# Layer 2's attention scores: three-part bfloat16 rows and one bfloat16 product in place of float32 products

## The chip, the cores and the metric

The kernel runs on one core of a Trainium2 chip. A core has a matrix engine (PE, whose weight loads are listed apart as PEld), a vector engine (DVE), a scalar engine (ACT), a general engine (POOL) and a queue that issues transfers (SP). Each engine works through its own instructions in a fixed order and waits on semaphores for what others make. Products land in PSUM[...]; everything else on the chip lies in SBUF. The metric is the device time of one execution, in microseconds (us); less is better.

## The reference

The input is 128 graphs of 128 nodes with 128 features, and an adjacency matrix for each. Four layers follow one another, each of the form x = x + gnn(relu(layernorm(x))). Layer 0 scores all pairs of nodes through a small network with a batch normalisation, layer 1 is an attention with eight heads and a second attention on top of it, layer 2 is a single attention, and layer 3 scores by edge type. Cut to what the change touches, layer 2 is

```python
f1 = h @ a1                       # h: [graph, node, 128], a1 and a2: [128, 1]
f2 = h @ a2
e = leaky_relu(f1 + swapaxes(f2, 1, 2), 0.2)
scores = where(adj > 0, e, -9e15)
attention = softmax(scores, axis=2)
return elu(attention @ h)
```

So the score of a pair of nodes is the sum of one number of each node, and everything after it (mask, exponential, weighted sum) starts from that.

## The kernel before

**Stages.** After a setup that loads and rearranges the weights, layer 0 takes about the first 2080 us. The function `layers` then does the rest of the network in one pass over 32 groups of four graphs (`GC` = 4). Nothing of this pass leaves the chip until a group's result is stored.

**The path of a group** is the generator `group`: layer 0's end, normalisation and transposition of h; values and scores of layer 1 by head (`pf`, `f`, `f1d`, `fl`, then `head_attention` for each graph, forked); ELU; a second attention (`z2`); normalisation; layer 2 (`z3`, `single_head`); normalisation; layer 3; store. In layer 2 the features `hv` are transposed into `h2T` (features on the partitions, four graphs side by side, 512 columns), ACT copies them out of PSUM (L953), and then line L1268 and its neighbours form the scores of the four graphs, key nodes on the partitions and query nodes in the columns, in one PSUM bank:

```python
yield PE, 2.0, "ps", "t"
z = psum("z3")
nc.tensor.matmul(z, a1bc, h2T, start=True, stop=False)
for i in range(GC):
    nc.tensor.matmul(z[:, i, :], h2T[:, i, :], a2c.to_broadcast([P, P]), start=False, stop=False)
masked(z, lambda: mask)
```

`a1bc` (L306) holds a1 in each of its 128 columns, so that the first product writes a query's f1 into every partition; the second, with a2 broadcast, adds a key's f2. `masked` (L958) adds a very large negative number where there is no edge, by a bfloat16 product of a scaled identity with the mask. In `single_head`, ACT then takes two exponentials of `z` (L970), with slopes 1 and 0.2, DVE takes their maximum (L962), and PE forms the weighted sum (L1006). A float32 product appears in the profile as two instructions, a bfloat16 product as one.

**Layer 1 has a form of its own for the same task.** `fw` holds the columns that give f1 and f2 of four heads, three times each, so that L1173 writes 24 rows per graph and half of the heads into a strip of 32 partitions. Four vector instructions (L1183 to L1186) then turn each set of three equal rows into three bfloat16 parts whose sum is the float32 number. The masks of rows `of_f1`, `of_f2` and `parts_m` say which row is which. L1194 writes rows with ones where the other factor stands, and L1068 multiplies, so that one bfloat16 product gives f1 + f2.

**What sets the order.** The instructions of PE, ACT, DVE and POOL are in an order written by a small planner, `in_order`, when the program is built. Each `yield` of a generator announces a step: its engine, an assumed cost in us, the buffers that it takes and those that it frees. The planner always picks the step that can begin first by its assumed costs, with six groups under way (`UNDER_WAY`) and a limited number of buffers of each kind: four PSUM banks of kind "ps", two pairs of banks "pz", 28 tiles "t", eleven "w", and so on. A changed cost or a new step therefore changes the order of all later steps. DMAs go through SP and POOL; each group's four inputs are loaded one group ahead.

Of the kernel before, what the change touches and what calls it, by code (L numbers as in the profile page):

```python
# [9 lines left out]
F32 = mybir.dt.float32  # L10
I32 = mybir.dt.int32
I16 = mybir.dt.int16
BF16 = mybir.dt.bfloat16
AF = mybir.ActivationFunctionType
ALU = mybir.AluOpType
AX = mybir.AxisListType
PSUM = bass.MemoryType.PSUM

P = 128
# [7 lines left out]
GC = 4  # L27
NH, DH = 8, 32
HH = NH // 2
# [3 lines left out]
C_T, C_W, C_V, C_O, C_M = 28, 11, 3, 6, 7  # L33
# [13 lines left out]
PE, ACT, DVE, POOL, DMA = "PE", "ACT", "DVE", "POOL", "DMA"  # L47
# [105 lines left out]
def bcast(ap, pos, n):  # L153

    dims = [list(d) for d in ap.ap]
    return bass.AP(tensor=ap.tensor, offset=ap.offset, ap=dims[:pos] + [[0, n]] + dims[pos:])
# [3 lines left out]
def kernel(ctx: ExitStack, tc: tile.TileContext, x, adj, w, out):  # L160
    nc = tc.nc
# [7 lines left out]
    def cst(name, shape, dtype=F32):  # L169
        return const.tile(shape, dtype, tag=name, name=name)  # L170

    ident = cst("ident", [P, P])
# [43 lines left out]
    w1c = cst("w1c", [P, NH, DH])  # L216
    fw = cst("fw", [P, 2, 32])
    w2g = cst("w2g", [P, 2, P + 2])
    a1bc = cst("a1bc", [P, P])
    a2c = cst("a2c", [P, 1])  # L220
    aq = cst("aq", [P, NT, P])
    aqb = cst("aqb", [P, NT])
    vpw = cst("vpw", [P, P])
    parts_m = cst("parts_m", [P, 2])
    of_f1 = cst("of_f1", [P, HH + 1])
    of_f2 = cst("of_f2", [P, HH + 1])
    one = cst("one", [P, 1])
    nc.vector.memset(one, 1.0)
    minus_one = cst("minus_one", [P, 1])
# [7 lines left out]
    with tc.tile_pool(name="wload", bufs=2) as wl, tc.tile_pool(  # L237
        name="wps", bufs=2, space=PSUM
# [24 lines left out]
        for m in range(2):  # L263
            prod = wl.tile([P, NH, DH], F32, tag="prod", name="prod")
            nc.vector.tensor_tensor(prod, w1c, a1b[:, :, m * DH : (m + 1) * DH], ALU.mult)
            for s in range(2):
                for k in range(3):
                    e = (3 * m + k) * HH
# [9 lines left out]
        for m, dst in ((0, of_f1), (1, of_f2)):  # L278
            rows = of_32[:, 3 * HH * m : 3 * HH * (m + 1)]
# [21 lines left out]
            nc.vector.tensor_reduce(gw, prod2, AX.X, ALU.add)  # L301
            nc.vector.tensor_copy(w2g[:, :, P + s], gw)

        acol = wl.tile([P, 1], F32, tag="acol", name="acol")
        nc.sync.dma_start(acol, w["L2_gnn_a1"])
        nc.vector.tensor_copy(a1bc, acol.to_broadcast([P, P]))  # L306
        nc.sync.dma_start(a2c, w["L2_gnn_a2"])


        araw = wl.tile([P, P, NT], F32, tag="araw", name="araw", bufs=1)  # L310
# [119 lines left out]
    with tc.tile_pool(name="h_pool", bufs=1) as h_pool, tc.tile_pool(name="pairs", bufs=B_V) as b_v:  # L430
# [10 lines left out]
        with tc.tile_pool(name="a2", bufs=2) as a2, tc.tile_pool(  # L441
            name="a_d", bufs=A_D
        ) as a_d, tc.tile_pool(name="a_ph", bufs=3, space=PSUM) as a_ph, tc.tile_pool(
            name="a_ps", bufs=2, space=PSUM
# [144 lines left out]
            with tc.manual_schedule(engines=ORDERED):  # L589
# [20 lines left out]
                start=True, stop=True,  # L610
# [12 lines left out]
        with tc.tile_pool(name="b2", bufs=2) as b2p, tc.tile_pool(name="b_s", bufs=2, space=PSUM) as b_s, tc.tile_pool(  # L623
            name="b_ps", bufs=6, space=PSUM
# [17 lines left out]
                start=True, stop=True,  # L642
# [228 lines left out]
            for k in [NB // GS - 1, *range(NB // GS - 1)]:  # L871
# [4 lines left out]
                n = 0 if makers else 2  # L876
# [12 lines left out]
    def layers(simple):  # L889

        with tc.tile_pool(name="c_in", bufs=3) as c_in, tc.tile_pool(
            name="c_t", bufs=C_T
        ) as c_t, tc.tile_pool(name="c_w", bufs=C_W) as c_w, tc.tile_pool(name="c_v", bufs=C_V) as c_v, tc.tile_pool(
            name="c_s", bufs=6
        ) as c_s, tc.tile_pool(name="c_ps", bufs=4, space=PSUM) as c_ps, tc.tile_pool(
            name="c_pz", bufs=2, space=PSUM
# [3 lines left out]
            def psum(name):  # L900
                return c_ps.tile([P, GC, P], F32, tag="ps", name=name)

            def psum2(name):
                return c_pz.tile([P, 2, 512], F32, tag="pz", name=name)
# [5 lines left out]
            def tile_t(name):  # L910
                return c_t.tile([P, GC, P], F32, tag="t", name=name)

            def tile_w(name):
                return c_w.tile([P, 8, P], F32, tag="w", name=name)
# [4 lines left out]
            def tile_s(name, n=GC):  # L919
                return c_s.tile([P, n], F32, tag="s" + name, name=name)  # L920
# [35 lines left out]
            def masked(z, get_mask):  # L956

                nc.tensor.matmul(z, ident_far, get_mask(), start=False, stop=True)  # L958

            def bounded(p, q):  # L960

                nc.vector.scalar_tensor_tensor(p, p, FLOOR, q, ALU.max, ALU.max)  # L962
# [93 lines left out]
            def head_values(pv, vals):  # L1056
# [3 lines left out]
                    pv.rearrange("p g (h d) -> p (g h) d", d=DH), AF.Identity, bias=one,  # L1060
                )

            def head_attention(i, f1d, fl, mask, vals, xh):
                yield PE, 0.7, "pz", ""
                z = psum2("z")
                for s in range(2):
                    r = 64 * (i % 2) + 32 * s
                    nc.tensor.matmul(  # L1068
                        z[:, s, :], fl[r : r + 32, i // 2, :], f1d[r : r + 32, i // 2],
                        start=True, stop=False, tile_position=(r, 0),  # L1070
                    )
                for s in range(2):
                    masked(z[:, s, :], lambda: bcast(mask[:, i, :], 1, NH // 2))
                yield ACT, 1.85, "w w", "pz"
                p, q = tile_w("p"), tile_w("q")
                by_bank = "p (s h) j -> p s (h j)"
                nc.scalar.activation(p.rearrange(by_bank, s=2), z, AF.Exp)  # L1077
                nc.scalar.activation(q.rearrange(by_bank, s=2), z, AF.Exp, scale=SLOPE)  # L1078
                yield DVE, 1.13, "", "w"
                bounded(p.rearrange("p h j -> p (h j)"), q.rearrange("p h j -> p (h j)"))  # L1080
                yield PE, 1.7, "ps", "w"

                pa_all = c_ps.tile([P, 512], F32, tag="ps", name="pa")
                pa = pa_all[:, 0 : NH * (DH + 1)].rearrange("p (h d) -> p h d", h=NH)
                vals_all = vals.rearrange("p g h d -> p (g h d)")
                for h in range(NH):
                    e = (i * NH + h) * (DH + 1)
                    n = min(WIDE, GC * NH * (DH + 1) - e)  # L1090
                    nc.tensor.matmul(  # L1091
                        pa_all[:, h * (DH + 1) : h * (DH + 1) + n], p[:, h, :], vals_all[:, e : e + n],
                        start=True, stop=True,
                    )
                yield DVE, 0.58, "", "ps"
                ri = tile_s("ri8", NH)
                nc.vector.reciprocal(ri, pa[:, :, DH])
                nc.vector.tensor_tensor(xh[:, i], pa[:, :, 0:DH], bcast(ri, 2, DH), ALU.mult)
# [24 lines left out]
            def group(g):  # L1123
# [36 lines left out]
                vals = c_v.tile([P, GC, NH, DH + 1], F32, tag="vals", name="vals")  # L1160
# [8 lines left out]
                pf = c_ps.tile([P, GC // 2, P], F32, tag="ps", name="pf")  # L1169
                for i in range(GC):  # L1170
                    for s in range(2):
                        r = 64 * (i % 2) + 32 * s
                        nc.tensor.matmul(  # L1173
                            pf[r : r + 32, i // 2, :], fw[:, s, :], h1T[:, i, :],
                            start=True, stop=True, tile_position=(0, r),
                        )
                yield DVE, 1.7, "", "ps"
                fa = c_v.tile([P, 2 * P], BF16, tag="fa", name="fa")
                fr = c_v.tile([P, 2 * P], F32, tag="fr", name="fr")
                fb = c_v.tile([P, 2 * P], BF16, tag="fb", name="fb")  # L1180
                f = c_v.tile([P, 2 * P], BF16, tag="f", name="f")
                pff = pf.rearrange("p s n -> p (s n)")
                nc.vector.tensor_copy(fa, pff)  # L1183
                nc.vector.scalar_tensor_tensor(fr, fa, parts_m[:, 0:1], pff, ALU.mult, ALU.add)
                nc.vector.tensor_copy(fb, fr)
                nc.vector.scalar_tensor_tensor(f, fb, parts_m[:, 1:2], fr, ALU.mult, ALU.add)  # L1186
                yield DVE, 0.8, "f w", ""
                fl = c_v.tile([P, 2, P], BF16, tag="fl", name="fl")
                f1d = c_v.tile([P, 2, HH, P], BF16, tag="f1d", name="f1d")
# [1 line left out]
                for h in range(HH + 1):  # L1191

                    m, c = (of_f1, of_f2) if h < HH else (of_f2, of_f1)
# [8 lines left out]
                mask = res["mask"]  # L1202
                xh = tile_w("xh").rearrange("p (g a) (b d) -> p g (a b) d", g=GC, d=DH)
                for i in range(GC):
                    yield "fork", head_attention(i, f1d, fl, mask, vals, xh)
# [25 lines left out]
                for i in range(GC):  # L1231
                    for s in range(2):
                        nc.tensor.matmul(  # L1233
                            ph2[:, i, 0 : P + 2], xcT[:, GC * s + i, :], w2g[:, s, :],
                            start=s == 0, stop=s == 1,
# [4 lines left out]
                z = psum("z2")  # L1240
                for i in range(GC):
                    nc.tensor.matmul(
                        z[:, i, :], h2[:, i, P : P + 1].to_broadcast([P, P]), ident,
                        start=i == 0, stop=False,
# [18 lines left out]
                h2T = []  # L1263
                yield from transposed(hv, h2T, "")
                h2T = h2T[0]
                yield PE, 2.0, "ps", "t"
                z = psum("z3")
                nc.tensor.matmul(z, a1bc, h2T, start=True, stop=False)  # L1268
                for i in range(GC):
                    nc.tensor.matmul(  # L1270
                        z[:, i, :], h2T[:, i, :], a2c.to_broadcast([P, P]), start=False, stop=False
                    )
                masked(z, lambda: mask)
                x3 = []
                yield from single_head(z, None, shift2, hv, P, x2, x3)
# [43 lines left out]
                p, q = tile_t("p3"), tile_t("q3")  # L1319
# [18 lines left out]
            load(1)  # L1338
            in_order(
                [partial(group, g) for g in range(NB // GC)], UNDER_WAY,  # L1340
                {"ps": 4, "pz": 2, "t": C_T, "w": C_W, "vals": C_V, "f": C_V, "v": C_O, "mask": C_M},
                C_KEPT,
            )

    with tc.If(nc.values_load(types[0:1, 0:1]) < 1) as only_01:
        layers(True)
    with only_01.Else():
        layers(False)
# [13 lines left out]
def program(arrays):  # L1362

    import concourse.bacc as bacc

    nc = bacc.Bacc("TRN2", target_bir_lowering=False, num_devices=1)
    ins, aps = {}, {}
    for name in ["x", "adj"] + _WEIGHTS:
        a = arrays[name]
        ins[f"in_{name}"] = a  # L1370
        aps[name] = nc.dram_tensor(
            f"in_{name}", a.shape, mybir.dt.from_np(a.dtype), kind="ExternalInput"
        ).ap()
    out = nc.dram_tensor("out_0", arrays["x"].shape, F32, kind="ExternalOutput").ap()
    with tile.TileContext(nc) as tc:
        kernel(tc, aps["x"], aps["adj"], aps, out)
    return nc, ins
# [10 lines left out]
```

## Time and profile before

| What | Value |
|---|---|
| median of three runs | 3178.52 us (3177.65 to 3181.38) |
| the profiled execution's own time | 3173.2 us |
| its span, first to last instruction | 3171.4 us |
| mean granted PE clock | 0.961 |
| PE busy over the span | 2832.2 us (89%) |
| DVE busy | 2657.7 us (84%) |
| ACT busy | 2673.4 us (84%) |
| POOL busy | 1495.2 us (47%) |
| L1268, 64 instructions of 512 columns | 33.8 us busy |
| L1270, 256 instructions of 128 columns | 33.7 us busy |

Busy times are unions of instruction durations. Matmuls overlap in the array, so a duration of 273 ns does not mean that the next one starts 273 ns later; where it matters, starts are compared with starts. Line numbers (L1268) are those of the kernel before. "Idle before, released by" names what ended a wait.

### The profile page before, as it was taken

To read this page: it belongs to the slowest core of one execution; us is meant where nothing else is said; L and a number is where in the kernel's file an instruction comes from. 1 tells how busy PE (TensorE), PEld (TensorE's weight loads), DVE (VectorE), ACT (ScalarE), POOL (GpSimd) and SP (SyncE) were. 2 spreads that over 40 slices of the span, in tenths; PEclk is the share of its full clock that TensorE was granted. 3 is DMA by queue.
4 is the path that set the end of the run, shared out by engine and by line. 5 is a ranking of instruction groups with operands and counts; after the bars stand their busy time and mean duration, and the time that the engine had idled before them with its cause. 6 is when DMAs were issued, how large, how long until landed. Compare 5 with 4: busy or idle time off the path is not lost.

```text
span 3171.4 us, 46611 instructions
## 1 busy us (share of the span) xinstructions
PE 2832.2 (89%) x17129; PEld 1559.5 (49%) x17129; DVE 2657.7 (84%) x4730; ACT 2673.4 (84%) x3082; POOL 1495.2 (47%) x953
## 2 busy tenths in 40 slices
PE   6999999999999998888888898789999999999996
PEld 2333333333333333233333333367777777877774
DVE  6999999999999998777787787667788878888864
ACT  5999999999999999987787887557877878887774
POOL 5999999999999996111111111122213222212211
PEclk8999999999999999999999998889999999999997
DMA  3555555555555550999999999420111111111000
GB/s 115 226 244 242 240 227 225 243 230 231 240 228 224 237 239 36 373 404 395 401 394 400 404 406 398 151 70 21 51 31 47 42 39 36 54 31 41 11 11 12
DMA packets 150718, 606.46 MB, mean 191 GB/s; under 512 B 15633, under 2 KB 99026, under 8 KB 119762
## 3 DMA queue, kind: packets, MB, share of 16 engines
q1 hardware_dynamic: 140242, 569.86, 45.6%
q0 software_dynamic: 10240, 33.53, 2.9%
q8 instruction: 139, 2.28, 0.3%
q14 instruction: 97, 0.79, 0.1%
HBM read 322.74 MB, written 280.61 MB: 190 GB/s over the span
## 4 chain that ended last, share of the span: by engine, by line
PE 27%; DVE 13%; issue 7%; ACT 5%; POOL 2%; DMA 1%; POOLq 0%; DVEq 0%; ACTq 0%
PE pa L1091 5%; PE sc L698 4%; PE po L1006 2%; DVE p L962 2%; PE z L958 1%; PE ps L1110 1%; PE pl L787 1%; PE pp L1103 1%; PE ph L1233 1%; DMA s<-us 1%; PE pl L789 1%; DVE s L928 1%; DVE v L425 1%; DVE xh L1015 1%; DVE f1d L1194 1%
## 5 line engine op out<-in xcount | busy, mean ns | idle before, releaser
L548 POOL TENSOR_TENSOR d<-he 128x2016 f32<-128x2016 f32 (+1 forms) x288 | 1022.0, 3578 | 77.6 <-ACT v L575 61.7
L565 PE MATMUL ph<-d,w1T 128*64 128x512 f32 (+1 forms) x4096 | 939.8, 596 | 83.1 <-ACT d L551 40.6
L551 ACT ACTIVATE d<-d 128x2016 f32<-128x2016 f32 (+1 forms) x384 | 741.1, 1932 | 0.1
L580 DVE BATCH_NORM_STATS2 six<-v 128x6 f32<-128x504 f32 (+1 forms) x1024 | 631.5, 670 | 8.7 <-ACT v L575 5.1
L565 PEld LDWEIGHTS ph<-d,w1T 128*64 128x64 f32 x4096 | 306.4, 136 | 613.7 <-issue 385.3
L575 ACT COPY v<-ph 128x1024 f32<-128x1024 f32 (+1 forms) x512 | 517.1, 1035 | 14.6 <-PE ph L565 14.6
L545 DVE TENSOR_TENSOR d<-he,pt 128x2048 f32<-128x2048 f32 (+1 forms) x224 | 506.1, 2259 | 13.0 <-PE ph L565 13.0
L935 POOL TENSOR_TENSOR rs<-ve,nhalf 128x4 f32<-128x4 f32 x96 | 120.0, 1250 | 772.2 <-DVE ve L932 558.1
L425 DVE SCALAR_TENSOR_TENSOR v<-v 128x1528 f32<-128x1528 f32 x256 | 433.9, 1742 | 32.8 <-ACT v L653 32.2
L653 ACT ACTIVATE v<-v,h_bi,h_sc 128x1528 f32<-128x1528 f32 x256 | 413.2, 1662 | 6.8 <-DVE h_bi L417 6.8
L698 PE MATMUL sc<-v,w_slide 128*32 128x512 f32 (+1 forms) x1536 | 321.4, 599 | 17.2 <-DVE v L425 16.9
L1091 PE MATMUL pa<-vals,p 128*128 128x99 f32 (+2 forms) x2048 | 254.9, 280 | 14.3 <-DVE p L962 11.1
L1091 PEld LDWEIGHTS pa<-vals,p 128*128 128x128 f32 x2048 | 249.2, 197 | 32.7 <-DVE p L962 15.1
L698 PE MATMUL sc<-v,w_line 128*32 128x504 f32 x512 | 260.3, 590 | 0.0
L698 PE MATMUL sc<-r,w_relu 128*32 128x504 f32 x512 | 258.2, 586 | 0.0
L962 DVE SCALAR_TENSOR_TENSOR p<-p,q 128x1024 f32<-128x1024 f32 (+1 forms) x192 | 206.2, 1081 | 49.5 <-ACT q L1078 24.9
L565 PE MATMUL ph<-both,us 128*64 128x512 bf16 x1536 | 190.5, 381 | 0.0
L1077 ACT ACTIVATE p<-z 128x1024 f32<-128x1024 f32 x128 | 133.2, 1040 | 35.0 <-PE z L958 34.5
L565 PEld LDWEIGHTS <-us 128*64 128x64 bf16 x1536 | 100.9, 111 | 117.7 <-issue 74.6
L660 ACT ACTIVATE r<-v,h_bi,h_sc 128x1008 f32<-128x1008 f32 x128 | 157.4, 1229 | 0.0
L799 ACT ACTIVATE e<-e 128x512 f32<-128x512 f32 x32 | 20.2, 630 | 149.3 <-DVE e L797 149.3
L698 PEld LDWEIGHTS sc<-v,w_slide 128*32 128x32 f32 x1536 | 65.1, 109 | 158.9 <-DVE v L425 82.5
(253 smaller groups left out, 4501.9 us busy)
## 6 DMA issues: line engine op xcount, KB each, us to landing
v<-v SPq DMA_DIRECT2D x240, 2032.0 KB, 9.1
xg<-in_x SPq DMA_DIRECT2D x64, 256.0 KB, 3.1
ht<-h SPq DMA_DIRECT2D x64, 256.0 KB, 6.4
u<-s POOLq DMA_DIRECT2D x16, 768.0 KB, 11.6
h<-he SPq DMA_DIRECT2D x32, 256.0 KB, 3.5
adj<-in_adj SPq DMA_DIRECT2D x32, 256.0 KB, 3.0
adj<-in_adj POOLq DMA_DIRECT2D x32, 256.0 KB, 8.6
y<-yt POOLq DMA_DIRECT2D x32, 256.0 KB, 7.1
```

The costliest lines, as they stand in the source:

```text
L425: engine.scalar_tensor_tensor(out, v, slope, v, ALU.mult, ALU.max)
L545: nc.vector.tensor_tensor(dv, later, own, ALU.subtract if q else ALU.max)
L548: nc.gpsimd.tensor_tensor(dv, later, own, ALU.subtract)
L551: nc.scalar.activation(d[:, 0 : 4 * n], d[:, 0 : 4 * n], AF.Abs)
L565: nc.tensor.matmul(ph[64 * a : 64 * a + 64, t, 0:n], wt, x_, start=part == 0, stop=q > 0 or part == 3,)
L575: nc.scalar.copy(v.rearrange("p (t e) -> p t e", t=2), ph[:, :, 0:n])
L580: nc.vector.bn_stats(made["six"][:, 2 * q + t, :], v[:, t * n : t * n + n])
L653: nc.scalar.activation(part, part, AF.Identity, bias=h_bi, scale=h_sc)
L660: nc.scalar.activation(made["r"][:, 0:n], part, AF.Relu, bias=h_bi, scale=h_sc)
L698: nc.tensor.matmul(sc[rows, 0:n], wz[:, 31 - k : 63 - k], z, start=begins and q < NQ, stop=ends and q != NQ - 1, tile_position=(0, rows.st ...
L962: nc.vector.scalar_tensor_tensor(p, p, FLOOR, q, ALU.max, ALU.max)
L1091: nc.tensor.matmul(pa_all[:, h * (DH + 1) : h * (DH + 1) + n], p[:, h, :], vals_all[:, e : e + n], start=True, stop=True,)
```

## The change

The columns a1 and a2 are no longer used alone. A new weight tile `fw2` of 32 columns holds a1 three times in its columns 0, 4, 8 and a2 three times in columns 12, 16, 20, so that the row masks of layer 1 fit. For each group, four float32 products (one per graph) with `fw2` as the stationary operand write a strip of 32 partitions each of a PSUM tile `pf2` of 128 columns. The four vector instructions that split rows into three bfloat16 parts become a helper, `in_parts`, which layer 1 calls as before and layer 2 calls for `pf2`. Five tensor_scalar instructions follow: one writes `fl2` (the f2 parts of the keys, and ones in the f1 rows), four write `f1g`, one per graph, with the f1 parts and ones in the rows of that graph and zeros in the rows of the other three (`own_f1`, `own_f2`). One bfloat16 product of `fl2` with the 512 columns of `f1g` then gives the scores of the four graphs, and the mask is added as before.

In the planner's terms, one step (PE 2.0) becomes four (PE 0.35, DVE 1.0, DVE 1.0, PE 0.5), with a new kind of buffer "g" of which there are two, and the PSUM kind "ps" is taken twice. In the setup, `a1bc` and its copy go, and `fw2`, `own_f1` and `own_f2` are filled by ten small vector instructions; both columns are still fetched by one DMA each.

```diff
-        acol = wl.tile([P, 1], F32, tag="acol", name="acol")
-        nc.sync.dma_start(acol, w["L2_gnn_a1"])
-        nc.vector.tensor_copy(a1bc, acol.to_broadcast([P, P]))
-        nc.sync.dma_start(a2c, w["L2_gnn_a2"])
+        nc.vector.memset(fw2, 0.0)
+        for m in range(2):
+            acol = wl.tile([P, 1], F32, tag="acol", name="acol")
+            nc.sync.dma_start(acol, w[f"L2_gnn_a{m + 1}"])
+            for k in range(3):
+                e = (3 * m + k) * HH
+                nc.vector.tensor_copy(fw2[:, e : e + 1], acol)
+        of_graph = wl.tile([P, GC], F32, tag="of_graph", name="of_graph")
+        nc.vector.tensor_reduce(of_graph, ident.rearrange("p (g k) -> p g k", k=32), AX.X, ALU.add)
+        for dst, rows in ((own_f1, of_f1), (own_f2, of_f2)):
+            nc.vector.tensor_scalar(dst, of_graph, rows[:, 0:1], None, ALU.mult)
...
+            def in_parts(rows, n, tag):
+                fa = c_v.tile([P, n], BF16, tag="fa", name="fa")
+                fr = c_v.tile([P, n], F32, tag="fr", name="fr")
+                fb = c_v.tile([P, n], BF16, tag="fb", name="fb")
+                f = c_v.tile([P, n], BF16, tag=tag, name="f")
+                nc.vector.tensor_copy(fa, rows)
+                nc.vector.scalar_tensor_tensor(fr, fa, parts_m[:, 0:1], rows, ALU.mult, ALU.add)
+                nc.vector.tensor_copy(fb, fr)
+                nc.vector.scalar_tensor_tensor(f, fb, parts_m[:, 1:2], fr, ALU.mult, ALU.add)
+                return f
...
-                yield PE, 2.0, "ps", "t"
+                yield PE, 0.35, "ps", "t"
+                pf2 = c_ps.tile([P, P], F32, tag="ps", name="pf2")
+                for i in range(GC):
+                    r = 32 * i
+                    nc.tensor.matmul(
+                        pf2[r : r + 32, :], fw2, h2T[:, i, :], start=True, stop=True,
+                        tile_position=(0, r),
+                    )
+                yield DVE, 1.0, "g", "ps"
+                f = in_parts(pf2, P, "f2")
+                yield DVE, 1.0, "", ""
+                fl2 = c_v.tile([P, P], BF16, tag="fl2", name="fl2", bufs=2)
+                f1g = c_v.tile([P, GC, P], BF16, tag="f1g", name="f1g", bufs=2)
+                nc.vector.tensor_scalar(
+                    fl2, f, of_f2[:, HH : HH + 1], of_f1[:, HH : HH + 1], ALU.mult, ALU.add
+                )
+                for i in range(GC):
+                    nc.vector.tensor_scalar(
+                        f1g[:, i, :], f, own_f1[:, i : i + 1], own_f2[:, i : i + 1], ALU.mult, ALU.add
+                    )
+                yield PE, 0.5, "ps", "g"
                 z = psum("z3")
-                nc.tensor.matmul(z, a1bc, h2T, start=True, stop=False)
-                for i in range(GC):
-                    nc.tensor.matmul(
-                        z[:, i, :], h2T[:, i, :], a2c.to_broadcast([P, P]), start=False, stop=False
-                    )
+                nc.tensor.matmul(z, fl2, f1g, start=True, stop=False)
                 masked(z, lambda: mask)
...
-                {"ps": 4, "pz": 2, "t": C_T, "w": C_W, "vals": C_V, "f": C_V, "v": C_O, "mask": C_M},
+                {"ps": 4, "pz": 2, "t": C_T, "w": C_W, "vals": C_V, "f": C_V, "g": 2, "v": C_O, "mask": C_M},
```

## The prediction

> **What bounds the kernel now.** I began with the page's share of busy time and its 40 slices, to find the stage that the change touches.
>
> ```profile
> PE 2832.2 (89%) x17129; PEld 1559.5 (49%) x17129; DVE 2657.7 (84%) x4730; ACT 2673.4 (84%) x3082; POOL 1495.2 (47%) x953
> PE   6999999999999998888888898789999999999996
> DVE  6999999999999998777787787667788878888864
> ```
>
> Layer 2 lies in the last 14 slices, from about 2080 us, where PE shows nines and DVE eights. I then cut this stage into stretches (columns: engine time, then busy us and count of PE, PEld, DVE, ACT, POOL, then clock and DMA).
>
> ```profile
> 2200.00:2400.00 200.00, 192.22 (x1436) 159.56 (x1436) 159.34 (x437) 155.46 (x280) 49.29 (x64) 0.97 0.15 43
> 2400.00:2600.00 200.00, 189.70 (x1430) 153.51 (x1431) 164.79 (x446) 159.32 (x282) 43.10 (x58) 0.99 0.14 41
> 2600.00:2800.00 200.00, 191.17 (x1442) 157.54 (x1441) 163.87 (x434) 162.68 (x285) 46.55 (x62) 0.99 0.16 44
> 2800.00:3000.00 200.00, 190.03 (x1456) 156.19 (x1456) 163.61 (x445) 157.68 (x285) 45.77 (x60) 0.99 0.09 27
> ```
>
> Over these 800 us PE is busy 763.1 (95%), DVE 651.6 (81%), ACT 635.1 (79%). The head exponentials come four to a group and their DVE line L962 (128x1024) 98 times here, so 24.5 groups pass, one per 32.65 us. Per group: PE 31.15 busy and 1.5 idle, DVE 26.6 busy and 6.05 idle, ACT 25.9 and 6.75. DMA is at 0.09 to 0.16 and plays no part. PE is first, DVE second by 4.5 us. Matching the k-th end of L962 with the k-th first matmul of L1091 in the trace, the operand lies ready 1.56 us (median) before PE takes it, and under 0.15 us in 18% of cases: PE is a queue that is usually behind. The list of waits in the window gives PE's idle time (us, times, longest):
>
> ```profile
> PE pa L1091 <- DVE p L962: 5.7, 8, 1.8
> PE z L1068 <- ACT q L1078: 5.7, 7, 1.4
> PE z L1268 <- ACT hTc L953: 4.2, 4, 2.1
> PE ptx L1220 <- DVE xc L1215: 3.2, 3, 1.7
> ```
>
> All entries together are 37 us; those on DVE are 14.2 (0.58 per group), those on ACT and the rest 0.92 per group.
>
> [...] the 16 narrow matmuls of L1173 together take 0.58 us (below), less than six ordinary ones at 0.11. [...] L1194's 256 elements start 0.257 us apart[...]. [...] L1194 has a median of 340 ns and a maximum of 1341.
>
> **The change part by part, PE.** Starts of successive lines on PE alone give what each step really occupies:
>
> ```profile
> 2403.70 1.12 PE L1268 MATMUL z<-hTc,a1bc 128*128 128x512 f32 x2 [2.06 <-ACT hTc L953]
> 2404.66 1.05 PE L1270 MATMUL z<-a2c,hTc 128*128 128x128 f32 x8
> 2405.56 0.38 PE L958 MATMUL z<-mask,ident_far 128*128 128x512 bf16 x1
> 2405.77 1.05 PE L1006 MATMUL po<-val,p 128*128 128x129 f32 x8
> ...
> 2711.06 0.64 PE L1173 MATMUL pf<-hTc,fw 128*32 128x128 f32 x16
> 2711.64 0.49 PE L1141 MATMUL po<-wtT,ht 128*128 128x128 f32 x2
> ```
>
> Removed: L1268, 0.96, and L1270, 0.90, here; 1.75 for both at 3138; I take 1.8. Added: eight narrow matmuls like half of L1173. Half of 0.58 is 0.29[...]; bounds 0.29 and 0.50, I take 0.38. Then one bfloat16 matmul of 512 columns like L958: 0.22. The mask product stays. PE saves 1.8 - 0.60 = 1.2 us per group (1.05 to 1.35), 38 us over 32 groups.
>
> **DVE.** The model is layer 1's same helper on twice the columns:
>
> ```profile
> 2097.44 0.42 DVE L1183 CAST fa<-pf 128x256 bf16<-128x256 f32 x1
> 2097.89 0.48 DVE L1184 SCALAR_TENSOR_TENSOR fr<-fa,parts_m,pf 128x256 f32<-128x256 bf16 x1
> 2098.40 0.29 DVE L1185 CAST fb<-fr 128x256 bf16<-128x256 f32 x1
> 2098.73 0.48 DVE L1186 SCALAR_TENSOR_TENSOR f<-fb,parts_m,fr 128x256 bf16<-128x256 bf16 x1
> 2099.14 1.11 DVE L1194 TENSOR_SCALAR f1d<-f,of_f,of_f 128x256 bf16<-128x256 bf16 x4
> 2100.16 0.34 DVE L1194 TENSOR_SCALAR fl<-f,of_f,of_f 128x256 bf16<-128x256 bf16 x1
> ```
>
> Steps of 0.45, 0.51, 0.33, 0.41, and 0.257 for each tensor_scalar. Halving the columns takes off 128 elements, 0.13 us at 1.04 ns each (L1015's 512 take 691 ns, L1098's 256 take 425)[...]: 0.32 + 0.38 + 0.26 + 0.28 = 1.24. A tensor_scalar of 128 lies between 0.13 (all of it elements) and 0.25 (all of it fixed)[...]. I take 0.21, so five are 1.05. [...] mean over median in this window is 0.06 for L1186, 0.05 for L1185, 0.02 to 0.04 for each L1194: 0.2. Sum 2.5 us per group (1.75 to 2.8), 80 us over 32 groups, none of it hidden by anything but DVE's 6.05 us gap. Behind these on DVE's in-order queue stand other groups' L962, L1215 and L1097/L1098, for which PE and ACT wait. The two planned steps (1.0 us each) can be separated by other work; inside one nothing can pass.
>
> **Buffers, order, ends.** The score step takes a PSUM slot of kind "ps" twice instead of once, but holds it for less matmul time (1.8 before, 0.6 after, plus 1.0 on DVE): about nothing. The new kind "g" has two slots, held from the first DVE step to the matmul; with one such stretch per 32 us it should not bind. fa, fr and fb are now used twice per group, but written and read on DVE alone. ACT, POOL and the queues of SP and POOL get nothing new in this stage; the planner moves all of their later steps by what it thinks saved. In the setup, both columns of a1, a2 are still fetched by two DMAs in the same place on SP. DVE gets ten small instructions for one (L306): they start 0.07 to 0.15 us apart, +0.9 us ahead of L313 at 19.71, whose result PE and the first statistics at 28.4 follow: +0.9 to the end. DVE now waits for the second column too, but that is issued at 14.1 and DVE comes by at 18.6. In the last group, the way from h2T to the exponential is 2.17 us (3138.36 to 3140.53); it becomes about 0.5 + 1.25 + 1.05 + 0.2 and the mask's 0.6: 3.5, so +1.3. The filling stretch before 2200, where the chain of waits lies more on DVE (54 us) than on PE (36), may give +1.5. Ends: +3.7.
>
> **The sum.** If PE's idle time stayed 1.5, the gain would be 1.2 x 32 = 38. But DVE's gap shrinks from 6.05 to about 3.0 of a 32 us period, and I let PE's waits for DVE grow as the gap shrinks: 0.58 x 6.05 / 2.95 = 1.19. Period: 31.15 - 1.2 + 0.92 + 1.19 = 32.06, against 32.65: -0.59 x 32 = -19. With the ends -15. The profiled execution took 3173.2 (span 3171.4, 1.8 around it), giving 3158; the median of the runs is 5.3 above it, so 3178.5 - 15 = 3164.
>
> **Rivals.** (1) PE is so far behind that all its saving is kept: -38 + 3.7, 3144. For it: the 1.56 us that operands lie ready. Against: DVE would have 29.1 of 31.5 us, 92%, next to a PE at 95%.
> (2) The window of six groups under way binds. A group lives 6 x 32.65 = 196 us; its path grows by 1.3 us and two more turns in PE's and DVE's queues at 1 to 2 us each, about 4 us or 2%, 0.65 per group, which cancels the 0.59: with the ends 3180, within 6 of before. Against: PE waits for nothing most of the time, so there is other work to take.
> (3) Slower: the DVE burst itself. L1194 is 2.4% of the chain of waits from 2080 to 3172 (26 us of its 160 x 0.257 = 41), so over 60% of such work lies on the path that ended last; L1268 and L1270 are on it with 37.5 of 58 us, 65%. If the new work did likewise, it costs 0.6 x 2.5 = 1.5 and the removal brings 0.65 x 1.2 = 0.8: +0.7 per group, which the planner's new order should soften to about 0.4: +13 + 3.7, 3195. It decides once PE's idle per group passes 1.5 + 1.2 - 0.1 = 2.6 us. Against: layer 1's f1d lies ready 8.7 us (median) before its matmul.
>
> **How the numbers follow.** Likeliest, part of the saving kept: 0.45, 3164, own range 3152 to 3172. All kept: 0.12. Cancelled: 0.15. Slower: 0.28. A difference under 0.2% (6.4 us) is about what this measurement cannot tell from none. So faster 0.57, same 0.15, slower 0.28. Range 3146 to 3194, which leaves out half of the all-kept case and the upper end of the slow one.
>
> **What would show it.** In the profile after: PE busy down by some 38 us in all; the narrow matmuls under 0.5 us from first start to the next line; DVE up by 70 to 85 us, with new tensor_scalar lines near 0.2 us apart; PE's share in the stretches falling from 95% to about 93% with DVE near 90%. PE's waits on DVE should about double from 14 us. Wrong if DVE's share stays under 86%, if PE idles more than 2.6 us per group, or if the exponentials of layer 2 wait on the new matmul for long.

## The result, and the profile after

The changed kernel takes 3205.55 us (median of 4 runs, 3200.07 to 3210.39), the kernel before beside it 3179.95 (3177.65 to 3183.29): ratio 1.0078, 95% interval 1.0063 to 1.0093. It is 25.6 us slower, outside the range of 3146 to 3194, on the side of the third rival. The profiled execution has a span of 3204.0 us.

The page's shares of the same engines (line numbers are now those of the changed kernel: L1091 was L1068, L1114 was L1091, L972 was L962, L968 was L958):

```profile
PE 2833.5 (88%) x17097; PEld 1544.8 (48%) x17097; DVE 2730.3 (85%) x5027; ACT 2674.4 (83%) x3082; POOL 1499.0 (47%) x953
```

DVE grew by 72.6 us, near the 80 of the forecast. PE did not shrink: 2833.5 against 2832.2, although 1.2 us of matmuls per group are gone. The stretches say the same (columns as before: the last three are PE's granted clock, the DMA share and GB/s):

```profile
2200.00:2400.00 200.00, 181.57 (x1384) 146.83 (x1384) 169.43 (x470) 152.33 (x272) 44.87 (x57) 0.97 0.15 42
2400.00:2600.00 200.00, 182.21 (x1392) 146.32 (x1391) 176.53 (x499) 158.08 (x282) 48.33 (x63) 0.98 0.14 41
2600.00:2800.00 200.00, 187.44 (x1388) 151.31 (x1387) 165.84 (x465) 151.55 (x269) 44.88 (x58) 0.94 0.13 37
2800.00:3000.00 200.00, 186.46 (x1412) 149.91 (x1411) 172.44 (x489) 156.03 (x278) 43.34 (x60) 0.96 0.13 37
```

PE is busy 737.7 of 800 us (92%), DVE 684.2 (86%). L972 (128x1024) comes 96 times, so 24 groups pass, one per 33.33 us instead of 32.65. Per group PE is busy 30.74 and idle 2.60, where 31.15 and 1.5 stood before. The waits of PE in that window (us, times, longest):

```profile
PE pa L1114 <- DVE p L972: 11.3, 9, 1.8
PE po L1016 <- ACT q L1101: 9.5, 8, 3.9
PE z L1304 <- DVE f1g L1299: 4.7, 7, 1.5
PE z L1091 <- ACT q L1101: 4.2, 5, 1.2
PE ptx L1235 <- DVE xc L1230: 4.0, 4, 2.0
```

All entries for DVE are 33.5 us against 14.2 before, those for ACT 25.0 against 18.9.

The new lines cost what was forecast. On DVE, one group's instructions with other groups' work between them:

```profile
2413.61 0.28 DVE L1080 CAST fa<-pf 128x128 bf16<-128x128 f32 x1
2413.93 0.35 DVE L1081 SCALAR_TENSOR_TENSOR fr<-fa,parts_m,pf 128x128 f32<-128x128 bf16 x1
2414.31 0.23 DVE L1082 CAST fb<-fr 128x128 bf16<-128x128 f32 x1
2414.57 0.35 DVE L1083 SCALAR_TENSOR_TENSOR f<-fb,parts_m,fr 128x128 bf16<-128x128 bf16 x1
2414.84 1.22 DVE L1230 SCALAR_TENSOR_TENSOR xc<-xc,xh 128x1024 f32<-128x1024 f32 x1
```

Steps of 0.32, 0.38, 0.26, 0.27; the five tensor_scalar start 0.22 us apart (median). On PE, the stretch from 2256 shows the narrow matmuls (L1285, 0.35 us to the next line), and what the forecast lacked:

```profile
2256.31 2.09 PE L1114 MATMUL pa<-vals,p 128*128 128x99 f32 x16 [1.81 <-DVE p L972]
2259.95 0.61 PE L1304 MATMUL z<-f1g,fl 128*128 128x512 bf16 x1 [1.54 <-DVE f1g L1299]
2260.35 0.63 PE L968 MATMUL z<-mask,ident_far 128*128 128x512 bf16 x1
2263.02 1.97 PE L1235 MATMUL ptx<-ident,xc 128*128 128x128 f32 x8 [2.04 <-DVE xc L1230]
...
2267.36 0.64 PE L1164 MATMUL po<-wtT,ht 128*128 128x128 f32 x2
2267.78 0.63 PE L1167 MATMUL po<-wtT,yl 128*128 128x128 f32 x2
...
2268.69 0.39 PE L1164 MATMUL po<-wtT,ht 128*128 128x128 f32 x2
2268.92 0.39 PE L1167 MATMUL po<-wtT,yl 128*128 128x128 f32 x2
...
2271.48 0.43 PE L1285 MATMUL pf<-hTc,fw 128*32 128x128 f32 x8
2271.83 0.44 PE L960 MATMUL pt<-ident,h 128*128 128x128 f32 x2
```

PE waits 1.81, 1.54 and 2.04 us for DVE, and from 2258.0 to 2268.3 the record of the granted clock (the share of full speed at which PE may run) has it at half: L1164 to L1167 is 0.42 us inside and 0.23 just after, L1304's 512 columns are 0.40 us instead of 0.21. In the two traces every stretch at half clock between 2200 and 3000 lasts 3.41 us or two or three times that, and all of a profile start on one grid of that step. Ahead of each of the ten slow windows of the changed kernel there, PE had been idle 1.0 to 2.9 us of the last 3.41. Together they last 58 us, against 20 us in five windows before, with 1.5 to 1.9 us of idle time ahead of each.

So I kept a ledger of the stage for each run's profiled execution, from its first product with `wtT` to the end: PE busy as it would be at full clock (busy time less half of what falls into slow windows, as 512 columns took 0.40 us there and 0.21 elsewhere), what the slow clock adds (that half), and PE idle. The stage of the changed kernel as one stretch (that of the kernel before stands with the experiments):

```profile
2078.10:3204.00 1125.90, 1013.53 (x7454) 809.72 (x7452) 922.51 (x2592) 830.54 (x1471) 241.56 (x319) 0.94 0.12 35
```

| us | stage | PE at full clock | slow clock adds | PE idle | DVE busy |
|---|---|---|---|---|---|
| before | 1102.3 | 986.1 | 31.5 | 84.7 | 850.5 |
| changed | 1125.9 | 959.8 | 53.7 | 112.4 | 922.5 |
| difference | +23.6 | -26.3 | +22.2 | +27.7 | +72.0 |

PE's saving is there. Idle time took it back once, and the clock that follows idle time once more. The spans of the two profiles differ by 32.6 us, though, and 9.0 of these lie ahead of the stage, where the work is the same apart from the setup; among the profiles of the work before alone, the stage starts anywhere from 2067.4 to 2079.3. A ledger is one execution, and executions of the kernel before range from 3167 to 3192 us, so a few us of any entry are scatter.

### The profile page after: what moved, and what is told of

Its sections match the earlier page's. It is cut to its first block, busy times and chain, and to the rows that moved or that the text cites. A ratio compares the mean times of both kernels' runs of the same rounds, so it can differ in the third digit from the quotient of the medians.

```text
span 3204.0 us, 46854 instructions
## 1 busy us (share of the span) xinstructions
PE 2833.5 (88%) x17097; PEld 1544.8 (48%) x17097; DVE 2730.3 (85%) x5027; ACT 2674.4 (83%) x3082; POOL 1499.0 (47%) x953
## 5 line engine op out<-in xcount | busy, mean ns | idle before, releaser
L1114 PE MATMUL pa<-vals,p 128*128 128x99 f32 (+2 forms) x2048 | 265.8, 287 | 20.7 <-DVE p L972 17.3
L1114 PEld LDWEIGHTS pa<-vals,p 128*128 128x128 f32 x2048 | 259.3, 204 | 45.1 <-DVE p L972 22.3
L972 DVE SCALAR_TENSOR_TENSOR p<-p,q 128x1024 f32<-128x1024 f32 (+1 forms) x192 | 203.3, 1065 | 37.1 <-ACT q L980 14.4
L805 DVE TENSOR_REDUCE mx<-pl 128x4 f32<-128x512 f32 x32 | 22.1, 691 | 148.5 <-PE pl L800 148.4
```

The source lines that it names most:

```text
L1114: nc.tensor.matmul(pa_all[:, h * (DH + 1) : h * (DH + 1) + n], p[:, h, :], vals_all[:, e : e + n], start=True, stop=True,)
```

## The experiments

Theory A: the vector work on DVE is what costs, through PE's waits. Theory B: the planner's new order is worse by itself. Theory C: PE's saving is void, since the clock falls. Each ratio is to runs of the kernel before that were measured beside it. Some of these kernels leave a part of layer 2's scores out, to separate the costs; their text says which.

**Each half alone.** PE's part without the nine vector instructions:

```diff
...
-                yield DVE, 1.0, "g", "ps"
-                f = in_parts(pf2, P, "f2")
-                yield DVE, 1.0, "", ""
-                nc.vector.tensor_scalar(
...
-                yield PE, 0.5, "ps", "g"
+                yield PE, 0.5, "ps", ""
-                nc.tensor.matmul(z, fl2, f1g, start=True, stop=False)
+                nc.tensor.matmul(z, ident_h, mask, start=True, stop=False)
```

> The changed kernel without its nine vector instructions per group: the narrow matmuls and one bfloat16 product of 512 columns stay, but the product reads the identity and the mask, so layer 2's scores do not depend on h. Theory A (the vector work is what costs; PE's saving is real): PE loses 1.2 us per group and nothing takes its place, 30 to 40 us under before, 3140 to 3152. Theory B (the planner's new order is worse by itself, whatever DVE does): no gain, 3175 to 3200. Theory C (PE's saving is void because PE's clock falls with any idle time): 3165 to 3180, with the slow clock windows of the changed kernel.

Measured: 3150.57 (3142.89 to 3152.75), ratio 0.9901 (0.9867 to 0.9934). In the ledger, PE at full clock 954.6, slow clock 29.1, idle 95.0: the saving stays and the clock with it. Theory C falls.

The vector part alone, on the kernel before:

```diff
+                yield DVE, 1.0, "g", ""
+                f = in_parts(h2T[:, 0, :], P, "f2")
+                yield DVE, 1.0, "", "g"
+                nc.vector.tensor_scalar(
...
                 yield PE, 2.0, "ps", "t"
```

> The kernel before with the nine vector instructions added per group ahead of the score step (their source is h2T, their results are not used) and the float32 products kept. Theory A: DVE gets 2.3 us per group and PE saves nothing; the changed kernel is 25 us slower with a saving of 30 to 40 in it, so this one is 45 to 75 us slower than before, 3225 to 3255. Theory B: the order decides, so anywhere within 20 us of before.

Measured: 3203.0 (3195.7 to 3212.12), ratio 1.0065 (1.0039 to 1.0091), 22 us slower: less than A asked, just past the 20 us of B, and the same as the changed kernel, which does 1.2 us less on PE per group. Either PE's saving is worth little beside the vector work, or one of the orders was a lucky one.

**Where the vector work goes.** The five tensor_scalar instructions on POOL:

```diff
-                yield DVE, 1.0, "", ""
+                yield POOL, 1.8, "", ""
-                nc.vector.tensor_scalar(
+                nc.gpsimd.tensor_scalar(
```

> The changed kernel with the five tensor_scalar instructions per group moved from DVE to POOL (planned at 1.8 us), which is 23% busy in this stage. Theory A: DVE keeps 1.25 of its 2.4 us per group, so about half of the 60 us that the vector work costs comes back: 3165 to 3185, unless POOL takes over 3 us for the five[...]. Theory B: no particular direction, 3180 to 3210.

Measured: 3225.73 (3223.86 to 3233.5), ratio 1.0149 (1.0115 to 1.0183). Slower, against A's number. The tile view of f1g in this run says why (its instruction on POOL: shortest, median and longest ns; then what PE waited for, us and times):

```profile
L1299 POOL TENSOR_SCALAR f1g<-f,own_f,own_f x128: 440/447/2460, 2152.2 to 3190.5; 128x128 bf16<-128x128 bf16 x128
  POOL f1g L1299: 31.5, 16
```

One takes 447 ns (median) and up to 2460, against 307 on DVE, and the score product waited 31.5 us for them, against 7.0 in the changed kernel. From the first start to the last end, the five took 3.1 us (median) and over 3 us in 18 of 32 groups, so the case that the expectation had excepted came true. On the theories the run says only that rows that come late enough starve PE.

**The order.** The old work in the order of the changed kernel's plan:

```diff
-                yield PE, 2.0, "ps", "t"
+                yield PE, 0.35, "ps", "t"
+                yield DVE, 1.0, "g", "ps"
+                yield DVE, 1.0, "", ""
+                yield PE, 0.5, "ps", "g"
                 z = psum("z3")
                 nc.tensor.matmul(z, a1bc, h2T, start=True, stop=False)
```

> The instructions of the kernel before in the order that the planner writes for the changed one: its four steps are announced, but the two vector steps and the first PE step are empty and the last PE step holds the float32 products. Theory A: the order leaves holes where the vector work was meant and overruns where the products come, but DVE has its gap back: 3180 to 3192. Theory B: the order carries the loss, 3200 to 3215.

Measured: 3212.77 (3210.16 to 3214.43), ratio 1.0102 (1.0071 to 1.0134). The order carries a loss here, of the size that B named. Its ledger has 102.1 us of PE idle and 47.6 us of slow clock, near those of the changed kernel, with no vector work added. But a plan that takes 2 us of products for 0.5, and holds h2T for free before they read it, is a poor plan for any work, so this run doesn't decide between the theories; it does show that an order alone can cost as much as the change. The next one is cleaner, one number in the kernel before:

```diff
-                yield PE, 2.0, "ps", "t"
+                yield PE, 1.8, "ps", "t"
```

> The kernel before, with one number changed: the planner is told 1.8 us instead of 2.0 for layer 2's score step (it takes 1.8 plus the mask's 0.2). The work is the same, only the order of later steps moves. Theory A (the vector work and the PE idle time that it brings are what costs): within 6 us of before. Theory B (any new order moves the time by as much as the change did): 10 to 30 us off, in either direction.

Measured: 3158.28 (3156.88 to 3161.81), ratio 0.9925 (0.9898 to 0.9951). With the same work it is 24 us faster than before, as much as the change lost, and it beats both kernels. The stage as a whole, from its first product with `wtT` to the end, as one stretch of the kernel before:

```profile
2069.10:3171.40 1102.30, 1017.61 (x7486) 828.09 (x7484) 850.51 (x2304) 829.47 (x1471) 237.87 (x319) 0.96 0.12 36
```

and the same stretch of this run:

```profile
2070.20:3156.80 1086.60, 1009.40 (x7487) 821.23 (x7484) 859.49 (x2304) 827.18 (x1471) 240.46 (x319) 0.97 0.12 36
```

PE at full clock is 988.2, as before; the slow clock adds 21.2 instead of 31.5, idle is 77.2 instead of 84.7. So theory B is true in part: an order alone moves the time by 0.7%. A single pair of kernels then proves nothing on the work, and I compared kinds of work over several orders.

The changed work in other orders. First the vector steps' measured costs:

```diff
-                yield DVE, 1.0, "g", "ps"
+                yield DVE, 1.3, "g", "ps"
...
-                yield DVE, 1.0, "", ""
+                yield DVE, 1.15, "", ""
```

> The changed kernel, with the planner told the measured costs of the two vector steps, 1.3 and 1.15 us in place of 1.0 and 1.0. Theory A: the work is the same and the plan a little truer, 3195 to 3207. Theory B: 10 to 30 us off the changed kernel's 3205 in either direction.

Measured: 3199.13, ratio 1.0052 (1.0030 to 1.0075). Then the vector work in seven small steps:

```diff
-                yield DVE, 1.0, "g", "ps"
+                yield DVE, 0.62, "g", "ps"
...
+                yield DVE, 0.55, "", ""
...
-                yield DVE, 1.0, "", ""
+                yield DVE, 0.22, "", ""
...
                 for i in range(GC):
+                    yield DVE, 0.22, "", ""
```

> The changed kernel with its vector work announced in seven steps of two or one instructions (0.62, 0.55 and five times 0.22 us) instead of two steps, so that the planner may put other groups' vector work in between. If the length of the burst in DVE's queue is what makes PE wait: 10 to 25 us less than the changed kernel, 3180 to 3195. If the amount of vector work is what counts: 3200 to 3210, as before the split.

Measured: 3200.59, ratio 1.0055 (1.0030 to 1.0080). The nine instructions do lie apart there (7.0 us from the first to the last, median, against 3.6 in the changed kernel), and the time is that of the other orders of this work. So the length of the burst isn't it. Then two costs of the second PE step:

```diff
-                yield PE, 0.5, "ps", "g"
+                yield PE, 0.3, "ps", "g"
```

> The changed kernel, planned cost of its second PE step 0.3 us instead of 0.5: another order for the changed work. If the vector work costs whatever the order: 3190 to 3215, with PE idle and slow clock in the stage near the changed kernel's 112 and 129 us. If only the changed kernel's order was bad: 3140 to 3175.

Measured: 3194.32, ratio 1.0048 (1.0025 to 1.0071).

and, in the same place, 0.7:

> The changed kernel, planned cost of its second PE step 0.7 us instead of 0.5: another order for the changed work. If the vector work costs whatever the order: 3190 to 3215. If only the changed kernel's order was bad: 3140 to 3175.

Measured: 3194.19, ratio 1.0054 (1.0038 to 1.0070).

The work before in other orders, planned at 1.6 and then at 2.2:

```diff
-                yield PE, 2.0, "ps", "t"
+                yield PE, 1.6, "ps", "t"
```

> The kernel before, planned cost of layer 2's score step 1.6 us instead of 2.0: a third order for the same work. If orders scatter around the kernel before, which happened to be ordinary: 3165 to 3195. If the kernel before had an unlucky order and others are like the one planned at 1.8: 3150 to 3168. With both changes of the step's cost the mean over orders of the work before is to be compared with the mean over orders of the changed work.

Measured: 3177.67, ratio 1.0004 (0.9988 to 1.0020).

> The kernel before, planned cost of layer 2's score step 2.2 us instead of 2.0: a fourth order for the same work. Ordinary scatter: 3165 to 3195. Unlucky order before: 3150 to 3168.

Measured: 3169.07, ratio 0.9960 (0.9948 to 0.9971).

**Amount or chain.** Is it the amount of vector work, or the longer chain PE, DVE, PE inside a group? First about half of the amount:

```diff
-                yield DVE, 1.0, "", ""
-                nc.vector.tensor_scalar(
...
-                nc.tensor.matmul(z, fl2, f1g, start=True, stop=False)
+                nc.tensor.matmul(z, f, mask, start=True, stop=False)
```

> The changed kernel without the five tensor_scalar instructions and their step: the split into parts stays, and the product takes the parts and the mask as operands, so layer 2's scores are not those of the reference. DVE keeps 1.25 of 2.4 us per group. Theory A with a cost in proportion to vector work: halfway between the run without vector work (3150) and the changed kernel (3205), 3172 to 3184. If the chain PE, DVE, PE inside a group is what costs, rather than its length: above 3190. Theory B: anywhere from 3150 to 3215.

Measured: 3177.12 (3166.2 to 3191.11), ratio 0.9983 (0.9966 to 1.0001), between the two, as in A. Then the chain with one short copy in place of the nine instructions:

```diff
-                yield DVE, 1.0, "g", "ps"
-                f = in_parts(pf2, P, "f2")
+                yield DVE, 0.35, "g", "ps"
+                f = c_v.tile([P, P], BF16, tag="f2", name="f")
+                nc.vector.tensor_copy(f, pf2)
...
-                nc.tensor.matmul(z, fl2, f1g, start=True, stop=False)
+                nc.tensor.matmul(z, f, mask, start=True, stop=False)
```

> The changed kernel with one vector copy of 128 columns (about 0.3 us) in place of the nine instructions; the score product waits for it and multiplies it with the mask, so the scores are not the reference's. If the amount costs: 3150 to 3165. If the chain costs: 3180 to 3200.

Measured: 3164.61, ratio 0.9953 (0.9939 to 0.9968). So with 0, 0.3, 1.25 and 2.3 us of vector work per group the changed kernel takes 3145 (mean of two orders, the second below), 3165, 3177 and 3198 (mean of six). The time rises with the amount, but not in proportion: the first 0.3 us cost 20, as much as the last 1.05. The two values in the middle are one order each, so whether that first step is the chain or the scatter of orders stays open. And all of the vector work as a branch that no score waits for:

```diff
+            def vector_work(pf2):
+                yield DVE, 1.0, "g", "ps"
+                f = in_parts(pf2, P, "f2")
+                yield DVE, 1.0, "", "g"
+                nc.vector.tensor_scalar(
...
+                yield "fork", vector_work(pf2)
+                yield PE, 0.5, "ps", ""
+                nc.tensor.matmul(z, ident_h, mask, start=True, stop=False)
```

> The changed kernel with all nine vector instructions kept, but as a branch of its own that nothing waits for; the score product reads the identity and the mask instead, so layer 2's scores do not depend on h. If the amount of vector work costs: near the changed kernel and its other orders, 3190 to 3205. If the chain inside a group costs: near the run without vector work, 3145 to 3165. Orders alone moved equal work by about 10 us either way.

Measured: 3228.9 (3226.53 to 3235.32), ratio 1.0152 (1.0130 to 1.0175). That is far from what the chain asked (3145 to 3165), but also 24 us above what the amount asked; the run doesn't show why, and it is one order. Taking the work off the scores' path brought nothing back, so the path is not the main cost. The waits say the same: in the changed kernel's whole stage PE waited 7.0 us for f1g, of 112.4 idle. Its stage as one stretch:

```profile
2079.00:3224.30 1145.30, 1023.91 (x7454) 818.75 (x7452) 929.33 (x2592) 830.15 (x1471) 234.63 (x319) 0.94 0.12 34
```

Ledger: PE at full clock 963.7, slow clock 60.2, idle 121.4. Seven groups under way, for the changed kernel and then for the one before:

```diff
-UNDER_WAY = 6
+UNDER_WAY = 7
```

> The changed kernel with seven groups under way instead of six. If a longer path per group in a window of six is what costs: 10 to 25 us less, 3175 to 3190. If DVE's load costs: 3190 to 3210, the scatter of orders.

Measured: 3191.9, ratio 1.0048 (1.0030 to 1.0066).

> The kernel before with seven groups under way instead of six, as the measure for the changed kernel with seven. No theory asks for a gain beyond the scatter of orders: 3155 to 3185.

Measured: 3169.37, ratio 0.9976 (0.9961 to 0.9992). Both gain about as much (0.30% and 0.24%), so the difference between them stays, 0.7%; the window of six isn't it.

**A second order for each half.** PE's part alone with its second step planned at 0.3 instead of 0.5:

```diff
-                yield PE, 0.5, "ps", ""
+                yield PE, 0.3, "ps", ""
```

> The run without vector work (scores from the mask alone) in a second order: the planned cost of its second PE step is 0.3 us instead of 0.5. The work before took 3158 to 3181 in five orders. If PE's saving is real when DVE is left alone: 3140 to 3160. If the first run was a lucky order: 3165 to 3180.

Measured: 3138.6 (3138.12 to 3139.58), ratio 0.9867 (0.9848 to 0.9886), just under the range for a real saving. The vector part alone with the score step planned at 1.8:

```diff
-                yield PE, 2.0, "ps", "t"
+                yield PE, 1.8, "ps", "t"
```

> The kernel before with the nine vector instructions added (results unused), in a second order: score step planned at 1.8 us. The changed work took 3192 to 3206 in six orders. If PE's saving counts beside the vector work: 3215 to 3240, 20 to 35 us above the changed work. If it counts for nothing there: 3192 to 3210, the same as the changed work.

Measured: 3223.16 (3211.65 to 3224.11), ratio 1.0121 (1.0089 to 1.0154), in the range for a saving of PE's that counts beside the vector work.

Mean ratios over the orders of each kind of work (runs with seven groups counted as orders), and the range of two ledger columns:

| work | orders | ratios | mean | PE idle, us | slow clock adds, us |
|---|---|---|---|---|---|
| before | 5 | 0.9925 to 1.0004 | 0.9973 | 77 to 85 | 21 to 32 |
| both parts (changed) | 6 | 1.0048 to 1.0078 | 1.0056 | 111 to 122 | 46 to 55 |
| PE part alone | 2 | 0.9867, 0.9901 | 0.9884 | 91, 95 | 24, 29 |
| vector part alone | 2 | 1.0065, 1.0121 | 1.0093 | 100, 112 | 43, 44 |

On 3180 us, from the mean of the work before: PE's part alone -28 us, the vector part alone +38, both +26. The ranges of before and changed don't overlap. The old work in the changed kernel's plan (1.0102) is left out as a poor plan; with it as a sixth order the mean of the work before would be 0.9995, the ranges would overlap, and the change would cost 19 us instead of 26. The sum of the halves would be +10; with two orders each and a scatter of about 10 us among orders, whether the missing 16 us are an interaction stays open.

## Why the prediction was wrong

**Sizes of the parts: right.** From the starts of lines, the narrow matmuls take 0.35 us (0.38 forecast, my estimate between two bounds) and the new product 0.21 (0.22), so PE saves 1.2 us per group; the ledger, which counts modelled durations, gives 0.8 over the whole stage, and 1.1 in the window from 2200 to 3000. DVE got 72 us (80 forecast), the tensor_scalar 0.22 us each (0.21, my estimate between 0.13 and 0.25); that the third vector step would shrink by 0.07 us and not by the 0.13 of 128 elements was an estimate too (0.26 forecast and measured). The PSUM slots, the kind "g", the setup and the end were not tested apart.

**The step that failed is the sum.** It had a period of 32.06 us; the profile has 33.33, and the miss of 1.27 times 32 groups is 41 us, which is 3205 less 3164. (The medians are meant; the two profiles put 23.6 us of the loss into the stage, where -15 was forecast.) Of the 1.27, 0.79 is PE's busy time, which came out at 30.74 instead of 29.95. I took a matmul's duration for fixed, but the clock fell after idle time: in this window the slow clock adds 1.08 us per group, against 0.41 before, which is 0.67 of the 0.79; the rest is that durations show a saving of 1.08 and not 1.2. The other 0.49 is idle time: the term for DVE was 1.19 and measured 1.40 (33.5 us over 24 groups), the rest was 0.92 and measured about 1.1 to 1.2. My estimate that PE's waits for DVE grow as DVE's gap shrinks was near; what I left out, and so put at nothing, is the slow clock that came with the idle time. In the ledger of this pair it is 0.8 us for each us of idle (22.2 to 27.7), over the means of six orders of the changed work and five of the work before 0.67 (22.8 to 34.1). It is no fixed price: PE's part alone idles 11 us more than the work before and has no more slow clock. In the profiles, half clock goes with how much idle time falls into one window of 3.41 us: it followed all 59 windows with 2.0 us or more and 1 of 1057 with less than 1.0 (last section). No run set the clock by itself.

**A second step was costed at nothing:** "the planner moves all of their later steps by what it thinks saved". New orders of the same work scatter over 0.8% for the kernel before. The kernel before lies 0.27% above the mean of its orders and the changed one 0.22% above its own, so by these orders this did not make the sign, but it is as large as the change and belonged in the range.

**The rivals and signs.** All saving kept (3144): true only with the vector work gone (3151 and 3139). The window of six: seven groups leave the difference as it was. Slower through DVE: right in sign, in size (3195 against 3205) and in the point from which it decides (2.6 us of PE idle per group; measured 2.60), but not in the mechanism as I put it. The burst costs no less in small steps, and the work costs no less off the scores' path. What is left is DVE's amount of work, with DVE at 86% beside PE at 92%: PE's waits for L972's maximum, which is old work, went from 5.7 to 11.3 us in the window. That the amount delays these results is the reading that fits the runs; the path of a single delay was not followed.

**The evidence that misled me:** operands of L1091 that lie ready for 1.56 us (median) before PE takes them; in the changed kernel it is still 0.99. The median describes the usual case; the cost came from the tail, where PE waits 1 to 2 us and then runs at half clock for 3.4 us or more. Two of the signs of being wrong came true, PE idle at 2.60 us per group and DVE's share under 86% (85.5); PE's busy time, which was to fall by 38 us, did not.

## What to carry to other kernels

When work moves from the busiest engine to the next one, add what both stand at afterwards: here 81% going to 86% on DVE cost more than a 4% saving on PE brought. On PE, idle time cost more than its length here, since half clock followed where it came crowded: 0.67 us more for each us, as a mean over orders. And where a planner writes the order, measure several orders of both versions before judging a change under one per cent: one number in an unchanged kernel gave 0.75%.

## What was not expected of the hardware

Half clock followed windows in which PE was idle for less than half of the time. From 2200 to 3000 us I cut each of the twenty profiles of this case into the windows of its own 3.41 us grid, and asked of every window at full clock in which PE was idle at all whether half clock followed:

| PE idle in the window, us | windows at full clock | followed by half clock |
|---|---|---|
| under 1.0 | 1057 | 1 |
| 1.0 to 1.5 | 193 | 14 |
| 1.5 to 2.0 | 110 | 73 |
| 2.0 and more | 59 | 59 |

The profiles of the two kernels alone give 1 of 100, 0 of 13, 9 of 15 and 5 of 5; after their 311 windows without idle time half clock never followed. So in this kernel the turn lies near 1.5 us of idle time within one window, in one piece or several: ahead of the ten slow windows of the changed kernel the longest single gap was 0.5 to 2.9 us. With 84.7 us of idle in the stage of the kernel before, the slow clock already added 31.5 us.

A tensor_scalar of 128 bfloat16 columns on DVE with two per-partition scalars still takes 307 ns (median of L1299) against 340 for 256 (L1194 of the kernel before), so halving the columns saved a tenth. The same instruction on POOL took 447 ns (median), at times 2460.
